# Rotary query halves swapped by transfers within SBUF, queries made three heads ahead

## The chip, the cores and the metric

The kernel runs on one core of a Trainium2 chip. The core has five engines that this text names: TensorE (PE, matrix products; its weight loads are listed apart as PEld), VectorE (DVE), ScalarE (ACT), GpSimd (POOL), and SyncE (SP), which in this kernel issues every transfer (DMA). Each engine works through its own queue in order; an instruction that waits holds up everything queued behind it on the same engine. Memory on the chip is SBUF (128 partitions) and PSUM, where PE leaves its sums.

The metric is the time of one execution in microseconds (us), median of several runs.

## The reference, cut to what matters

The reference is a two-block transformer with 4 sequences of 512 tokens and 1024 features: a first attention without weights, a mixture of low-rank experts, a second attention with low-rank queries and keys, and a second feed-forward. The change touches only the queries of the second attention, which has 32 heads:

```python
q = _rmsnorm(x @ wq_a.T, q_a_ln_w) @ wq_b.T
q = q.reshape(B, S, H, QHD)                       # 32 heads, 64 + 64 wide
q_nope, q_pe = (q[..., :NOPE], q[..., NOPE:])
q_pe = _apply_rope(_deinterleave(q_pe), cos, sin)  # x*cos + rotate_half(x)*sin
q_full = jnp.concatenate([q_nope, q_pe], axis=-1)
scores = jnp.einsum('bqhd,bkhd->bhqk', q_full, k_full) * softmax_scale
attn = jax.nn.softmax(where(causal, scores), axis=-1)
```

`rotate_half` takes 64 features to (minus the upper 32, the lower 32). For each of 32 heads and 4 sequences, a 64 x 512 block of the query is multiplied by a table of cosines, its two halves of 32 are exchanged and multiplied by a table of signed sines, and the two products are added.

## The kernel before

The kernel has four stages: the first attention, the first feed-forward, the heads of the second attention, and the second feed-forward (with the last output projection). The heads stage is a loop over 128 units `u`: 4 groups of 8 heads, 4 sequences per group, 8 heads each. A query lies transposed, 128 features on the partitions and 512 tokens along the free axis: features 0 to 63 are the part without rotation, 64 to 95 (`lo_`) and 96 to 127 (`hi_`) the two rotary halves, both together `mid`.

One query goes through these steps:

- `query(u)`: six matrix products of 512 columns (lines 150 to 152) leave it in the PSUM tile `psq`, of which there is one buffer. Every product of this kernel is made in three passes, from operands that are split into a high part and a low part.
- `rotate_query(u)`: ACT copies it to the SBUF tile `qf` (line 728, two buffers). DVE makes `t2` (the profile calls it `t`) from the PSUM tile with two multiplications of 32 partitions each, which read one half and write the other (lines 730 and 731). POOL multiplies `qf[mid]` by the cosines in place (line 732) and adds `t2` (line 733).
- `split_query(u)`: DVE casts columns 128 to 511 to the high part `qh` (line 740), POOL takes the low part `ql` by subtraction (line 741).
- `scores(u)`: four blocks of scores of 512, 384, 256 and 128 columns. The first product of each block reads `ql` (line 150), the last block reads `qf` (line 912). DVE adds the causal mask and takes the row minimum (line 918), ACT takes the exponential (line 921). The score tile `pss` has two buffers, so the third block waits until DVE is done with the first.
- `turn(u)` (line 942, copies at line 944) transposes the probabilities, `context(u)` (line 958, multiplication at 961) multiplies them by the keys' low-rank form for a pair of heads.
- `divisors(u)` sends the row sums through DRAM and back (`r_d`, `rb`, lines 887 and 891).

A "filler" is interleaved into the loop so that PE has work between the steps of a head: `project` (output projection of the previous sequence; operands added by DVE at line 984, cast by ACT at 992 and split by POOL into `cxl` at 993; sums added by DVE at 1035; its tiles `xs` loaded and stored by SP at lines 1020 and 1039) and `prepare_output` for the weights of a group.

The loop body of unit `u` has this order: two blocks of scores of `u`, a step of `context`, filler, `split_query(u + 1)`, two more blocks of scores, transposes of `u - 1`, filler, `query(u + 2)`, `rotate_query(u + 2)`, filler, transposes, and the loads: at the third head of a sequence `load_batch` fetches the next sequence's low-rank queries `q_d` (1 MB, line 699), keys `kT` (512 KB, line 701) and two smaller tensors. Queries 0 and 1 are made before the loop, at the end of the preceding projection stage; unit 0 makes query 2.

Inside this stage the order in each engine's queue isn't the written order: a planner simulates the program, keeps the data dependencies and lets an engine take the earliest written instruction that is ready by its own estimate of durations, transfers included. The order that results is then fixed; the engines wait by semaphores.

Of the kernel before, what the change touches and what calls it, by code (L numbers as in the profile page):

```python
# [17 lines left out]
P = 128  # L18
# [28 lines left out]
def block_kernel(ctx: ExitStack, tc: tile.TileContext, a: dict, out: bass.AP):  # L47
# [400 lines left out]
    wA = []  # L448

    def split_shared(pool, ch):  # L450
        r = rawA[:, ch * NA : (ch + 1) * NA]
        h, l = (pool.tile([P, NA], FR, name=f"wA{ch}{k}") for k in "hl")
        A.copy(h, r)
        G.tensor_tensor(l, r, f32(h), ALU.subtract)
        wA.append((h, l))
# [192 lines left out]
    ropeT = cc.tile([P, 2, S], F32, name="ropeT")  # L648
    nc.sync.dma_start(out=ropeT[NOPE:P], in_=a["ropeT"])
# [75 lines left out]
    def rotate_query(u):  # L725
        ps = queries[u]
        f = qp.tile([P, S], F32, name="qf")
        A.copy(f, ps)  # L728
        t2 = qp.tile([P, S], F32, name="t2", bufs=1)
        V.tensor_tensor(t2[lo_], ps[hi_], ropeT[hi_, 1, :], ALU.mult)  # L730
        V.tensor_tensor(t2[hi_], ps[lo_], ropeT[lo_, 1, :], ALU.mult)  # L731
        G.tensor_tensor(f[mid], f[mid], ropeT[mid, 0, :], ALU.mult)  # L732
        G.tensor_tensor(f[mid], f[mid], t2[mid], ALU.add)  # L733
        queries[u] = f

    def split_query(u):
        f = queries[u]
        h = qp.tile([P, S - P], FR, name="qh")
        l = qp.tile([P, S - P], FR, name="ql")
        V.tensor_copy(h, f[:, P:S])  # L740
        G.tensor_tensor(l, f[:, P:S], f32(h), ALU.subtract)  # L741
        queries[u] = f, h, l

    wqs, batches = {}, {}
    with tc.tile_pool(name="c1_w", bufs=1, side="right") as wap, \
# [73 lines left out]
        for s in range(NT + 1):  # L819
# [12 lines left out]
            if s in (NT - 2, NT - 1):  # L832
                query(s - NT + 2, pwp, "po")
                rotate_query(s - NT + 2)
# [10 lines left out]
    with ExitStack() as c2:  # L845
# [368 lines left out]
        for u in range(NU + 3):  # L1214
# [9 lines left out]
            if b == 0 and i == (HG // 2 if g else 0) and g < NG:  # L1224
                filler = prepare_output(g, wo_raw)
            sc = scores(u) if u < NU else iter(())
# [7 lines left out]
            if u + 1 < NU:  # L1234
                split_query(u + 1)

            if u == 0:
                query(2, psq, "psq")
            advance(sc)
# [10 lines left out]
            if 0 < u < NU - 2:  # L1250
                query(u + 2, psq, "psq")
            if u + 2 < NU:
                rotate_query(u + 2)
# [418 lines left out]
def _laid_out(i):  # L1672
# [8 lines left out]

    signed_T = np.concatenate([sin[:, :half], -sin[:, half:]], axis=1)
# [25 lines left out]
        "ropeT": np.stack([cos.T, signed_T.T], axis=1),  # L1708
# [21 lines left out]
```

## Time and profile before

| what | value |
|---|---|
| median of 3 runs | 1747.93 us (1747.41 to 1749.18) |
| span of the profiled execution, first to last instruction | 1746.3 us |
| heads stage in it (first rotated query's copy to the last unit's scores) | 414 to 1480 us |
| PE, DVE, ACT, POOL busy over the span | 98%, 75%, 52%, 53% |
| ACT copy of a query (line 728) | 587 ns, 126 of 128 from `psq` |
| DVE multiplications of the halves (730, 731) | 696 and 691 ns, 128 each |
| POOL cosine multiplication, addition, low part (732, 733, 741) | 1285, 1284 and 1013 ns, 128 each |

The profile is one execution of its own. Its page gives the span; its time from outside is the span and what lies around it, and isn't listed apart. The median of the three timed runs is 1.6 us above this span. Engines' busy times are sums of instructions; PE's instructions are pipelined and overlap, so a PE that is listed as busy can still lose time between two products. Waits are listed by the engine that stood still and the instruction that released it; "issue" means that nothing visible held it.

### The profile page before, as it was taken

What the parts mean: (1) busy time and instruction counts of PE and PEld (TensorE: products, weight loads), DVE (VectorE), ACT (ScalarE), POOL (GpSimd) and SP (SyncE); (2) the same over time, 40 slices, a digit from 0 to 9 for tenths busy, and PEclk for the clock granted to TensorE, in tenths of its full rate; (3) what the DMA queues carried; (4) which work ended last, traced back from release to release, by engine and by line L of the source; (5) the groups of instructions that cost most, each with busy time, mean ns of one, the idle gap of its engine ahead of it and who ended that gap; (6) DMA issues with size and microseconds to landing.
All of it is one profiled execution on the core that took longest, in us unless ns stands there. A gap on an engine that the chain in (4) does not pass through costs nothing.

```text
span 1746.3 us, 31628 instructions
## 1 busy us (share of the span) xinstructions
PE 1707.5 (98%) x10536; PEld 1429.7 (82%) x10536; DVE 1302.4 (75%) x3494; ACT 905.0 (52%) x2316; POOL 921.9 (53%) x926
## 2 busy tenths in 40 slices
PE   7999999999999999999999999999999999999999
PEld 6899999998677777767777767777767777789998
DVE  7977885676777777787777687777778776687675
ACT  7422331366765555575555575555476555453332
POOL 0553541203665665566566556566556655675454
PEclk9999999999999999999999999999999999999999
DMA  4313543245334234353333353342454333853431
GB/s 194 135 42 115 185 159 114 89 138 169 106 99 140 81 118 140 113 172 117 110 112 119 110 193 95 106 139 94 131 169 151 102 110 109 309 201 123 137 105 74
DMA packets 131939, 228.16 MB, mean 131 GB/s; under 512 B 22272, under 2 KB 58752, under 8 KB 128448
## 3 DMA queue, kind: packets, MB, share of 16 engines
q1 hardware_dynamic: 131776, 226.13, 39.2%
q8 instruction: 84, 1.38, 0.3%
q14 instruction: 79, 0.65, 0.1%
HBM read 156.60 MB, written 71.83 MB: 131 GB/s over the span
## 4 chain that ended last, share of the span: by engine, by line
PE 88%; DVE 5%; POOL 4%; ACT 2%; issue 1%; DMA 0%; POOLq 0%; ACTq 0%; DVEq 0%
PE psv L958 8%; PE pst L942 7%; PE po L150 4%; PE po L152 4%; PE po L151 4%; PE pss L150 4%; PE pss L151 3%; PE pss L152 3%; PE pob L150 3%; PE poa L150 3%; PE psq L150 3%; PE psq L152 3%; PE psq L151 3%; PE acc L150 3%; PE acc L152 3%; PE acc L151 3%
## 5 line engine op out<-in xcount | busy, mean ns | idle before, releaser
L921 ACT ACTIVATE p<-p,mn 128x512 f32<-128x512 f32 (+3 forms) x512 | 284.9, 559 | 211.4 <-DVE mn L918 210.8
L732 POOL TENSOR_TENSOR qf<-qf,ropeT 64x512 f32<-64x512 f32 x128 | 164.4, 1285 | 259.1 <-ACT qf L728 249.3
L918 DVE CUSTOM_DVE_ANT_0 p<-pss,causal 128x512 f32<-128x512 f32 (+3 forms) x512 | 232.7, 485 | 19.8 <-PE pss L152 15.8
L942 PE MATMUL pst<-ident,p 128*128 128x128 f32 x1280 | 185.9, 273 | 1.8 <-ACT pT L944 1.7
L733 POOL TENSOR_TENSOR qf<-qf,t 64x512 f32<-64x512 f32 x128 | 164.3, 1284 | 32.0 <-DVE t L731 23.8
L942 PEld LDWEIGHTS pst<-ident,p 128*128 128x128 f32 x1280 | 153.0, 141 | 29.6 <-ACT pT L944 4.8
L944 ACT COPY pT<-pst 128x512 f32<-128x512 f32 x256 | 142.1, 579 | 31.4 <-PE pst L942 29.5
L741 POOL TENSOR_TENSOR ql<-qf,qh 128x384 fp32r<-128x384 f32 x128 | 129.6, 1013 | 53.0 <-DVE qh L740 53.0
L150 PE MATMUL pss<-kT,ql 128*128 128x512 f32 (+2 forms) x384 | 143.6, 374 | 4.4 <-POOL ql L741 4.2
L993 POOL TENSOR_TENSOR cxl<-s,cxh 128x256 fp32r<-128x256 f32 x128 | 98.1, 773 | 85.2 <-ACT cxh L992 53.9
L150 PE MATMUL po<-w_h,hTl 128*128 128x384 f32 (+1 forms) x384 | 133.1, 347 | 0.7 <-DVE x L433 0.6
L151 PE MATMUL pss<-kT,qh 128*128 128x512 f32 (+2 forms) x384 | 130.4, 340 | 0.0
L152 PE MATMUL po<-w_h,hTh 128*128 128x384 f32 (+1 forms) x384 | 130.1, 339 | 0.0
L152 PE MATMUL pss<-kT,qh 128*128 128x512 f32 (+2 forms) x384 | 129.9, 338 | 0.0
L151 PE MATMUL po<-w_l,hTh 128*128 128x384 f32 (+1 forms) x384 | 129.7, 338 | 0.0
L944 DVE COPY pT<-pst 128x256 f32<-128x256 f32 x128 | 54.1, 423 | 97.8 <-PE pst L942 97.2
L728 ACT COPY qf<-psq 128x512 f32<-128x512 f32 x126 | 73.9, 587 | 69.7 <-PE psq L152 68.0
L730 DVE TENSOR_TENSOR t<-psq,ropeT 32x512 f32<-32x512 f32 x126 | 87.7, 696 | 24.5 <-ACT qf L728 20.2
L921 ACT ACTIVATION_READ_ACCUMULATOR p<-p,mn 128x1 f32 x512 | 97.2, 190 | 0.0
L150 PEld LDWEIGHTS pss<-kT,ql 128*128 128x128 f32 x384 | 72.1, 188 | 29.1 <-POOL ql L741 9.2
L731 DVE TENSOR_TENSOR t<-psq,ropeT 32x512 f32<-32x512 f32 x126 | 87.1, 691 | 1.7
L1035 DVE TENSOR_TENSOR xs<-xs,pob 128x512 f32<-128x512 f32 x105 | 71.1, 677 | 19.0 <-PE pob L152 18.8
(567 smaller groups left out, 4975.0 us busy)
## 6 DMA issues: line engine op xcount, KB each, us to landing
xs<-x_d SPq DMA_DIRECT2D x128, 256.0 KB
x_d<-xs SPq DMA_DIRECT2D x128, 256.0 KB
slotC<-in_woT_dram SPq DMA_DIRECT2D x32, 512.0 KB
rb<-r_d SPq DMA_DIRECT2D x128, 128.0 KB
w_t<-raw SPq DMA_DIRECT2D x32, 288.0 KB
x<-in_x_dram SPq DMA_DIRECT2D x16, 512.0 KB
x_d<-x SPq DMA_DIRECT2D x32, 256.0 KB
slotA<-q_d SPq DMA_DIRECT2D x8, 1024.0 KB
```

The source lines that it names most:

```text
L150: T.matmul(ps, lhsT=al, rhs=bh, start=start, stop=False, **kw)
L151: T.matmul(ps, lhsT=ah, rhs=bl, start=False, stop=False, **kw)
L152: T.matmul(ps, lhsT=ah, rhs=bh, start=False, stop=stop, **kw)
L732: G.tensor_tensor(f[mid], f[mid], ropeT[mid, 0, :], ALU.mult)
L733: G.tensor_tensor(f[mid], f[mid], t2[mid], ALU.add)
L741: G.tensor_tensor(l, f[:, P:S], f32(h), ALU.subtract)
L918: turn_of[0] = V.tensor_tensor_reduce(out=to, in0=ps[:, 0:n], in1=causal[:, S - n : S], scale=1.0, scalar=-NEG, op0=ALU.add, op1=ALU.min, ...
L921: A.activation(to, to, AF.Exp, bias=mn[:, i : i + 1], scale=-1.0, accum_out=rs[:, i : i + 1])
L942: T.transpose(ps[:, w : w + P], p[:, OF[i] + j * P : OF[i] + (j + 1) * P], ident)
L944: copy(pT[:, AT[js[0]] : AT[js[0]] + w], ps[:, 0:w])
L958: T.matmul(ps[n * KVR : (n + 1) * KVR, S - w : S], lhsT=k[:, j, :], rhs=pTs[u + n][:, AT[j] : AT[j] + w], start=(j == 0), stop=(j == TPB - 1))
L993: G.tensor_tensor(l, src, f32(h), ALU.subtract)
```

## The change

- `ropeT` is now laid out over 128 partitions: the signed sines on partitions 0 to 63, the cosines on 64 to 127 (256 KB as before).
- `rotate_query` exchanges the halves by two transfers from `qf` to partitions 0 to 63 of `t2`, 32 partitions of 2 KB each (64 KB per transfer), issued on SP. One DVE multiplication then reads `t2[0:64]` and the sines, both in SBUF, and writes `t2[64:128]`. POOL's cosine product goes to a tile of its own, and POOL adds the two products into `qf`. The PSUM tile is read by ACT alone.
- `qf` has three buffers. The loop makes and rotates `query(u + 3)` in unit `u` (unit 0 makes queries 2 and 3), and `split_query(u + 1)` stands ahead of the scores of `u`.
- The POOL tile shares its place with the weight tile `wA0` of the projection stage, whose two halves become one tile.

```diff
     def split_shared(pool, ch):
         r = rawA[:, ch * NA : (ch + 1) * NA]
-        h, l = (pool.tile([P, NA], FR, name=f"wA{ch}{k}") for k in "hl")
+        both = pool.tile([P, 2, NA], FR, name=f"wA{ch}")
+        h, l = both[:, 0], both[:, 1]
...
-    ropeT = cc.tile([P, 2, S], F32, name="ropeT")
-    nc.sync.dma_start(out=ropeT[NOPE:P], in_=a["ropeT"])
+    ropeT = cc.tile([P, S], F32, name="ropeT")
+    nc.sync.dma_start(out=ropeT, in_=a["ropeT"])
...
-    def rotate_query(u):
+    def rotate_query(u, pool=None):
         ps = queries[u]
-        f = qp.tile([P, S], F32, name="qf")
+        f = qp.tile([P, S], F32, name="qf", bufs=3)
         A.copy(f, ps)
         t2 = qp.tile([P, S], F32, name="t2", bufs=1)
-        V.tensor_tensor(t2[lo_], ps[hi_], ropeT[hi_, 1, :], ALU.mult)
-        V.tensor_tensor(t2[hi_], ps[lo_], ropeT[lo_, 1, :], ALU.mult)
-        G.tensor_tensor(f[mid], f[mid], ropeT[mid, 0, :], ALU.mult)
-        G.tensor_tensor(f[mid], f[mid], t2[mid], ALU.add)
+        nc.sync.dma_start(out=t2[0:32], in_=f[hi_])
+        nc.sync.dma_start(out=t2[32:NOPE], in_=f[lo_])
+        V.tensor_tensor(t2[mid], t2[0:NOPE], ropeT[0:NOPE], ALU.mult)
+        tc_ = (pool or firstp).tile([P, S], F32, name="wA0", bufs=1)
+        G.tensor_tensor(tc_[mid], f[mid], ropeT[mid], ALU.mult)
+        G.tensor_tensor(f[mid], tc_[mid], t2[mid], ALU.add)
         queries[u] = f
...
                 query(s - NT + 2, pwp, "po")
-                rotate_query(s - NT + 2)
+                rotate_query(s - NT + 2, wk)
...
+            if u + 1 < NU:
+                split_query(u + 1)
             sc = scores(u) if u < NU else iter(())
...
             advance(filler, per[0])
-            if u + 1 < NU:
-                split_query(u + 1)
 
             if u == 0:
                 query(2, psq, "psq")
+                rotate_query(2)
...
-            if 0 < u < NU - 2:
-                query(u + 2, psq, "psq")
-            if u + 2 < NU:
-                rotate_query(u + 2)
+            if u + 3 < NU:
+                query(u + 3, psq, "psq")
+                rotate_query(u + 3)
...
-        "ropeT": np.stack([cos.T, signed_T.T], axis=1),
+        "ropeT": np.concatenate([signed.T, cos.T]),
```

## The prediction

> **What bounds the kernel now.** I read the page's first and fourth parts, then the heads stage alone: busy time by stretch, the waits of PE and of its weight loads, the instructions on the query's tiles, and SP's waits.
>
> ```profile
> span 1746.3 us, 31628 instructions
> PE 1707.5 (98%) x10536; PEld 1429.7 (82%) x10536; DVE 1302.4 (75%) x3494; ACT 905.0 (52%) x2316; POOL 921.9 (53%) x926
> PE 88%; DVE 5%; POOL 4%; ACT 2%; issue 1%; DMA 0%; POOLq 0%; ACTq 0%; DVEq 0%
> ```
>
> PE is busy nearly all the time, and 88% of the chain that ended last runs on it. The second answer is a table by stretch (stretch, length, then busy time and instruction count of PE, PEld, DVE, ACT, POOL):
>
> ```profile
> 465.00:700.00 235.00, 232.78 (x1307) 178.07 (x1306) 175.40 (x474) 136.05 (x377) 143.92 (x140) 1.00 0.36 116
> 940.00:1200.00 260.00, 258.84 (x1432) 197.00 (x1431) 193.89 (x513) 152.39 (x416) 158.54 (x155) 1.00 0.38 122
> ```
>
> In the heads stage PE is idle 2.2 us in 235 and 1.2 us in 260. So nothing that DVE, POOL or ACT saves is time in itself; only what makes PE wait counts. The weight-load and matmul waits of the stage (414 to 1480 us; total, times, longest):
>
> ```profile
> PEld pss L150 <- POOL ql L741: 9.2, 23, 1.5
> PEld pst L942 <- ACT pT L944: 4.4, 6, 0.8
> PEld pob L150 <- POOL cxl L993: 3.8, 12, 0.7
> PE pss L150 <- POOL ql L741: 4.2, 8, 1.2
> PE pst L942 <- ACT pT L944: 1.7, 4, 0.4
> PE pob L150 <- POOL cxl L993: 0.9, 3, 0.3
> ```
>
> The largest wait with a named cause is the first: a head's scores stand still for `ql`, the low part of their query. The timeline shows why: POOL makes `ql` at 914.19 to 915.20 us, and the scores that read it start at 915.25. The query's chain ends just in time.
>
> **The change, part by part.** The sum is made against the profiled span, 1746.3 us; the median of the runs is 1.6 us above it, and I add that at the end.
>
> *A query made three heads ahead.* 118 query copies lie between 465 and 1466 us: 1001/118 = 8.5 us per head. The rotation moves a head forward and the split to the start of the preceding head. Every instruction of the rotation moves with it: the ACT copy, the transfers, the DVE multiplication, both POOL operations; six products on PE are made earlier, not more often. `ql` then has about 8.5 us to spare less what the new chain takes longer (below). The waits for `ql`: 9.2 us of weight loads, in the same places as the 4.2 us of matmuls, so between 4.2 and 13.4; I take 9.2, because a held weight load delays the product by itself. From 465 us on 6.1 us of it lie (19 times), before that 3.1 us (4 times). Gain: 6.1 in the steady part. What is late next there is `cxl` (3.8 + 0.9 us listed, and 1.9 on the other output bank), which this part doesn't help.
>
> *The start.* Queries 0 and 1 gain no lead: their rotation is still the last thing before their scores. Of the 3.1 us before 465, I let 1.5 go (heads 2 to 5, which do gain) and charge heads 0 and 1 for the longer chain.
>
> *The transfers.* SP issues 2 more transfers per query, 256 in all; transfer issues here take 0.33 us (`x_d` stores) to 0.54 us (`rb`), so 0.66 to 1.08 us per query and 84 to 138 us of SP's time. SP waits far longer than that:
>
> ```profile
> SPq L887 <- DVE rt L883: 171.6, 56, 10.3
> SPq L1039 <- DVE mn L918: 142.9, 29, 11.6
> SPq L699 <- PE psv L958: 104.5, 14, 9.6
> SPq L1020 <- DMA x_d<-xs: 61.9, 60, 3.4
> ```
>
> (465 to 1466 us.) Behind the new issues stand loads and stores of `xs`, the `r_d`/`rb` round trip and the batch loads. They come up to 1.1 us later. `rb` of one pair is issued at 908.69 and multiplied in by DVE at 919.10, the `xs` loads stand still for earlier stores anyway. I take 0, with 0 to +3 us as its ends: were that cover gone, 1.1 us on each of some three dozen `xs` loads would show through 0.1 us at a time.
>
> No row shows how long a transfer inside SBUF takes. The nearest is `r_d`: its fourth issue ends at 924.27 and the `rb` issue, which waits for it, starts at 925.23, so at most 0.96 us to land 1 KB. For 128 KB I add 0.4 us at the fastest slice of the page (309 GB/s) to 1.0 us at its mean (131 GB/s). Issue and landing together: 2.0 to 3.0 us behind the copy, if nothing larger is in front; a 1 MB `q_d` load in front adds up to 1024 KB/309 GB/s = 3.4 us, a 512 KB load 1.7 us. A landing at once would be the other end; 2.3 us is what I take, nearest to the `r_d` row.
>
> *One multiplication instead of two.* The rows (min/median/max ns):
>
> ```profile
> L730 DVE TENSOR_TENSOR t<-psq,ropeT x126: 695/696/697, 426.1 to 1468.6; 32x512 f32<-32x512 f32 x126
> L731 DVE TENSOR_TENSOR t<-psq,ropeT x126: 690/691/692, 426.8 to 1469.3; 32x512 f32<-32x512 f32 x126
> L984 DVE TENSOR_TENSOR s<-a,a x16: 679/811/1328, 1506.8 to 1718.0; 128x512 f32<-128x512 f32 x16
> ```
>
> Two times 0.69 = 1.39 us go, each with one operand in PSUM and a flat duration. The new one has both operands in SBUF; the nearest row for that form and length is the third, 0.68 to 1.33 us, median 0.81. Saved per head: 0.06 to 0.71 us, I take 0.55; over 128 heads 70 us of DVE's time, 8 to 91 as ends. It is hidden, since DVE isn't the bound. What it moves: now the mask of the first score block stands behind both multiplications (908.61 + 0.69, then the mask at 909.33, although its scores were done near 908.1), and the third block's products wait for that mask. Waits of weight loads on DVE in the whole stage are small (mask 2.6 and 2.4 us, `cx` 2.4, `rt` 2.4), together 9.8 us. I take a gain of 2, between 0 and 9.8.
>
> The SBUF page of the Trainium skill ("SBUF — State Buffer", section "Who interferes with whom") speaks against this edit: a Vector instruction with two SBUF inputs contends with a GpSimd instruction that reads SBUF, one with at most one such input doesn't. The spread of the third row beside the flat first two agrees. By its exclusive lock the new multiplication could stand behind a whole POOL operation and take 1.28 us more, which would make the pair's replacement dearer than the pair by about 0.6 us per head. The rows' bound above doesn't need it.
>
> *POOL* has the same three instructions per head, 1285 + 1284 + 1013 ns; the added tile changes no size. `t2` is ready 2.3 + 0.8 = 3.1 us after the copy instead of 1.6 us (copy ends 907.87, second multiplication 909.30), so the addition starts some 1.5 us later. In the steady part that is paid from the 8.5 us. For heads 0 and 1 it is paid in full: 2 x 1.5 = 3, less what PE can fill in with query 2 or 3; the second also has a 1 MB and a 512 KB load in front of it (issued at 416.80 and 418.32, its copy near 420). I take +2, ends 0 and 5.
>
> *What queues behind the new wait.* On DVE the multiplication waits for the landing, and masks, casts, sums and copies stand behind it; on POOL the addition waits for DVE, with `cxl` and `ql` behind. The planner puts both where its own estimate lands the transfer, so only a later landing costs, and a mask has the 1.39 us of the removed multiplications to give. I take +2 for landings behind big loads; ends 0 and +23, the latter worked out as the first rival.
>
> Sum: -6.1 - 1.5 + 2 - 2 + 0 + 2 = -5.6, so a span of 1740.7 and a median of about 1742.5 us. The ends that lower it: 13.4 instead of 7.6 for `ql`, 9.8 instead of 2 for DVE.
>
> **The rivals.** First, slower: *DVE stands on the swap.* Large loads in the stage: 16 of 1 MB, 16 of 512 KB keys, 32 of 512 KB `slotC`. If a swap meets one, it lands 3.4 or 1.7 us late. Less 1.4 us of slack that is 2.0 and 0.3 us at DVE's queue: 16 x 2.0 + 48 x 0.3 = 46 us if all meet, 23 us if half do, and PE, which has no reserve, shows it. 1742.5 - 2 + 23 = 1763.5. For it: PE's few waits mean that every new one counts, and SP stands still two thirds of the time (its eleven largest waits sum to 667 of 1001 us), so a swap could also queue behind a store that isn't ready (up to 11.6 us). Against it: DVE is idle a quarter of the stage, its own waits there (94 us on transposes) cost PE almost nothing. It decides once DVE's lateness costs PE more than the 7.6 us gained: 0.06 us per head.
>
> Second, no difference: *the wait is replaced.* `ql` is no longer late, but `cxl` is, since POOL's addition now lies about where `cxl` is split (the split at 911.97 would fall into an addition from about 911.0 to 912.3). 0.3 us more on a third of the 128 units, less those with spare operands: +5, so 1747.5. For it: 6.6 us of such waits are there already. Against it: the filler makes its operands two steps ahead.
>
> Third, a larger gain: *all named waits shrink.* `ql` 13.4, DVE 9.8 by half, `cxl` by half: 13.4 + 4.9 + 6.6/2 - 2 (the charge at the start) = 19.6 at most, 14 more than the forecast's 5.6; half way there is 1742.5 - 7 = 1735.5. For it: DVE loses 70 us of work, and the query's PSUM tile is free after the copy, so the planner can fill PE's gaps with a query. Against it: PE's idle time in the steady stretches is barely 6 us in 1001.
>
> **How the numbers follow.** 0.2%, 3.5 us, is about what a measurement of this kernel can tell from no change: below 1744.4 is faster, above 1751.4 slower. Chances: forecast 0.42, DVE stands on the swap 0.34, wait replaced 0.14, larger gain 0.10. The forecast's own range is 1737 to 1746.5; a fifth of it (0.08) lies within 3.5 us of before, and of the slow rival 0.02 does. Faster 0.34 + 0.10 = 0.44; same 0.14 + 0.08 + 0.02 = 0.24; slower 0.32. The range of 8 in 10 leaves out the lower half of the larger gain (0.05) and the slow rival beyond its worked price (0.13): 1734 to 1764.
>
> **What would show it.** Right: the wait of the scores on `ql` gone but for the first two heads; DVE busy down by about 70 us in the heads stage and its multiplication near 0.8 us; the mask of the first block no longer behind a multiplication; PE's busy time unchanged, the stage shorter by 4 to 8 us. Wrong: DVE idle in front of the new multiplication, released by the transfer, for more than 1 us in many heads; masks late behind it and weight loads of the third score block waiting on them; or `cxl` waits above 10 us. The prediction fails most easily by the landing time of the swap, which no row shows.

## The result and the profile after

The changed kernel takes 1773.66 us (median of 4 runs, 1773.17 to 1775.28) beside 1748.33 us for the kernel before on the same chip: 1.0145 times as long, 95% interval 1.0133 to 1.0158. The forecast was 1742.5 us in a range of 1734 to 1764; it was wrong in sign, and the time lies 9.7 us above the range.

The page's first part and the chain, after:

```profile
span 1771.4 us, 32282 instructions
...
PE 1703.4 (96%) x10536; PEld 1431.8 (81%) x10536; DVE 1246.9 (70%) x3366; ACT 907.9 (51%) x2316; POOL 939.5 (53%) x926
...
PE 59%; POOL 5%; DVE 4%; issue 2%; DMA 1%; ACT 1%; SPq 0%; POOLq 0%; ACTq 0%; DVEq 0%
```

DVE lost 55.5 us of work, as the edit promised. PE is no busier, yet the span is 25.1 us longer: PE stood still. The shares of the chain that are listed sum to 72%, so I read from it only that PE's listed share fell from 88 to 59%.

Two tables by stretch show where (stretch, length, busy time and instruction count of PE, PEld, DVE, ACT, POOL, then the granted clock, the DMA share and GB/s). Before, for the start of the heads stage, which the prediction didn't show:

```profile
414.00:465.00 51.00, 48.09 (x264) 34.36 (x263) 37.55 (x117) 37.14 (x101) 31.44 (x28) 1.00 0.45 140
```

After:

```profile
421.00:465.00 44.00, 34.36 (x160) 23.96 (x161) 21.50 (x71) 24.31 (x65) 19.82 (x17) 0.92 0.36 105
465.00:700.00 235.00, 230.21 (x1315) 176.82 (x1315) 163.04 (x455) 141.79 (x389) 153.21 (x143) 1.00 0.42 133
784.30:799.60 15.30, 12.18 (x58) 9.02 (x58) 10.38 (x23) 8.77 (x21) 10.80 (x11) 0.89 0.31 97
800.00:1030.00 230.00, 228.50 (x1285) 178.85 (x1285) 158.02 (x425) 126.65 (x352) 144.07 (x140) 1.00 0.43 134
```

PE idles 9.6 us in the first 44, 3.1 us in 15 around 790, and 1.5 us in the 230 us after that. The loss is in a few places. To see them all, I take for each head the time of its last score product (line 915 after, 912 before) and subtract the same of the kernel before. The lag is 5.2 us at head 0, 16.0 at head 9, then falls to 13.0 at head 43, is 19.0 at head 47, 23.2 at head 79, 28.1 at head 111, and 24.6 at the last. So there is a start that costs 16 us, three jumps between heads 43 and 47, 75 and 79, 107 and 111, each at the same head of a group, and between them a slow gain. At the start and at the jumps the filler is `prepare_output`: the output weights of a group are made from loads into `slotC`, on PE, ACT, DVE and POOL.

What PE and its weight loads waited for from 421 to 1480 us (total, times, longest):

```profile
PE pss L150 <- POOL ql L744: 21.9, 12, 3.4
PE pss L150 <- DVE mn L921: 9.9, 10, 2.7
PE pob L150 <- POOL cxl L996: 1.6, 3, 0.6
PEld pss L150 <- POOL ql L744: 26.7, 18, 3.7
PEld pss L150 <- DVE mn L921: 15.1, 19, 3.1
```

The scores wait for `ql` in fewer places than before (18 weight loads instead of 23), but for three times as long in all, and for a mask that is late, which they hardly did before:

```profile
PEld pss L150 <- DVE mn L918: 2.6, 7, 0.8
```

`cxl` is not late.

What DVE, POOL and SP waited for in the same time:

```profile
DVE qh L743 <- POOL qf L736: 114.8, 119, 2.0
DVE t L733 <- DMA t<-qf: 13.7, 19, 1.7
POOL qf L736 <- DVE t L733: 54.9, 51, 3.8
SPq L731 <- ACT qf L729: 115.9, 55, 4.7
SPq L731 <- POOL qf L736: 70.2, 30, 6.6
SPq L1049 <- PE pst L945: 10.3, 4, 3.3
```

The second line is the wait that the first rival was built on. It is small: DVE met an unfinished transfer 19 times, 1.7 us at most. The swap is late further up, on SP: 30 times it waits for POOL's addition (line 736), since `t2` has one buffer and the addition is its last reader. The sixth line is a load into `slotC` that waits for its room, and the jump at head 44 shows what that does. SP's queue there (start, duration, issue):

```profile
772.65 0.97 SPq L890 DMA_DIRECT2D r_d<-rt  x3
776.66 0.83 SPq L1049 DMA_DIRECT2D slotC<-in_woT_dram  x2
...
778.45 0.51 SPq L731 DMA_DIRECT2D t<-qf  x1
...
788.64 0.54 SPq L731 DMA_DIRECT2D t<-qf  x1
```

ACT's copy of query 44 ended at 772.50. SP stood 3 us on the `slotC` load, issued it, and reached the swap at 778.45, 5.95 us behind the copy. What followed on DVE, POOL and PE:

```profile
786.42 0.69 DVE L733 TENSOR_TENSOR t<-t,ropeT 64x512 f32<-64x512 f32 x1
...
787.32 1.29 POOL L736 TENSOR_TENSOR qf<-wA,t 64x512 f32<-64x512 f32 x1 [3.00 <-PE pst L945]
788.65 0.36 DVE L743 CAST qh<-qf 128x384 fp32r<-128x384 f32 x1 [0.82 <-POOL qf L736]
...
788.70 1.45 POOL L735 TENSOR_TENSOR wA<-qf,ropeT 64x512 f32<-64x512 f32 x1
790.22 1.26 POOL L1091 TENSOR_TENSOR b221l<-raw,b221h 128x512 fp32r<-128x512 f32 x1
791.45 0.99 POOL L744 TENSOR_TENSOR ql<-qf,qh 128x384 fp32r<-128x384 f32 x1
...
792.49 0.50 PE L150 MATMUL pss<-kT,ql 128*128 128x512 f32 x1 [3.12 <-POOL ql L744]
```

The multiplication stands in DVE's queue behind a head's masks and divisors and runs 7.4 us after the start of the swap's second issue; the addition frees `t2` at 788.61 and the next swap is issued 0.03 us later; `ql` stands on POOL behind the next query's cosine product and a weight's low part; PE stands 3.12 us. From copy to the end of `ql` this took 19.9 us, where the kernel before took 5.4. Every step is an engine that works its queue in order, and every wait is handed on.

### The profile page after: what moved, and what is told of

Read it like the earlier page. It is cut to its first block, busy times and chain, and to the rows that moved or that the text cites. A ratio compares the mean times of both kernels' runs of the same rounds, so it can differ in the third digit from the quotient of the medians.

```text
span 1771.4 us, 32282 instructions
## 1 busy us (share of the span) xinstructions
PE 1703.4 (96%) x10536; PEld 1431.8 (81%) x10536; DVE 1246.9 (70%) x3366; ACT 907.9 (51%) x2316; POOL 939.5 (53%) x926
## 4 chain that ended last, share of the span: by engine, by line
PE 59%; POOL 5%; DVE 4%; issue 2%; DMA 1%; ACT 1%; SPq 0%; POOLq 0%; ACTq 0%; DVEq 0%
PE psv L961 8%; PE pst L945 6%; PE pss L150 4%; PE pss L151 3%; PE pss L152 3%; PE pob L150 3%; PE poa L150 3%; PE psq L152 3%; PE psq L150 3%; PE psq L151 3%; PE acc L150 3%; PE acc L152 2%; PE acc L151 2%; PE poa L152 2%; PE poa L151 2%; PE pob L152 2%
## 5 line engine op out<-in xcount | busy, mean ns | idle before, releaser
L736 POOL TENSOR_TENSOR qf<-wA,t 64x512 f32<-64x512 f32 x128 | 165.0, 1289 | 115.5 <-DVE t L733 54.9
L735 POOL TENSOR_TENSOR wA<-qf,ropeT 64x512 f32<-64x512 f32 x128 | 169.4, 1323 | 58.4 <-ACT qf L729 50.2
L151 PE MATMUL pss<-kT,qh 128*128 128x512 f32 (+2 forms) x384 | 133.0, 346 | 0.0
L152 PE MATMUL pss<-kT,qh 128*128 128x512 f32 (+2 forms) x384 | 131.2, 342 | 0.0
L743 DVE CAST qh<-qf 128x384 fp32r<-128x384 f32 x128 | 46.1, 360 | 116.9 <-POOL qf L736 116.9
L733 DVE TENSOR_TENSOR t<-t,ropeT 64x512 f32<-64x512 f32 x128 | 109.0, 852 | 19.0 <-DMA t<-qf 15.2
L996 POOL TENSOR_TENSOR cxl<-cx,cxh 128x256 fp32r<-128x256 f32 x96 | 76.8, 803 | 84.9 <-ACT cxh L995 78.8
```

The costliest lines, as they stand in the source:

```text
L151: T.matmul(ps, lhsT=ah, rhs=bl, start=False, stop=False, **kw)
L152: T.matmul(ps, lhsT=ah, rhs=bh, start=False, stop=stop, **kw)
L735: G.tensor_tensor(tc_[mid], f[mid], ropeT[mid], ALU.mult)
L736: G.tensor_tensor(f[mid], tc_[mid], t2[mid], ALU.add)
L996: G.tensor_tensor(l, src, f32(h), ALU.subtract)
```

## The experiments

All times are medians; "before" is 1747.7 to 1748.8 us in all groups. The reference in the tables is the second kernel of the first group, 1742.86 us: three heads ahead, rotation as before. Lags are differences of the last score product of a head between two profiled executions.

### Which part costs

Three parts can be taken one by one: the rotation (new: transfers and one multiplication; old: two multiplications out of PSUM), the heads of lead, and the place of the split. With the old rotation and a third `qf`, the sines were put on partitions 0 to 63 to make room.

The split put back:

```diff
-            if u + 1 < NU:
-                split_query(u + 1)
             sc = scores(u) if u < NU else iter(())
...
             advance(filler, per[0])
+            if u + 1 < NU:
+                split_query(u + 1)
```

> The changed kernel with the split of the next query put back behind the second score block, where it was before; transfers, one multiplication and three heads ahead stay. Theory S (the cast, queued ahead of the masks, makes VectorE stand on GpSimd's addition: 116.9 us of such waits against 15.1 before): the stand falls to under 40 us, the start's loss of 16 us and most of the three jumps of 6.6 us go, the small steady gain stays: 1735 to 1750. Theory R (the rotation by transfers is what comes late: the swap waits for the one buffer t2, and the addition stands in GpSimd's queue): 1765 to 1780, as the changed kernel (1773.7). Theory L (three heads ahead by itself upsets the order): the same 1765 to 1780.

The lead taken back to two heads, besides:

```diff
             if u == 0:
                 query(2, psq, "psq")
-                rotate_query(2)
...
-            if u + 3 < NU:
-                query(u + 3, psq, "psq")
-                rotate_query(u + 3)
+            if 0 < u < NU - 2:
+                query(u + 2, psq, "psq")
+            if u + 2 < NU:
+                rotate_query(u + 2)
```

> Transfers and the one multiplication alone: queries two heads ahead and the split at its old place. S: no early cast, so no loss but also little lead for ql; 1742 to 1752. R: the longer rotation has now one head less of lead, so its lateness shows in full: 1775 to 1800, TensorE waiting on ql for over 60 us. L: 1742 to 1752.

The old rotation with the new lead and split, and with the old split:

```diff
-        f = qp.tile([P, S], F32, name="qf")
+        f = qp.tile([P, S], F32, name="qf", bufs=3)
...
-        V.tensor_tensor(t2[lo_], ps[hi_], ropeT[hi_, 1, :], ALU.mult)
-        V.tensor_tensor(t2[hi_], ps[lo_], ropeT[lo_, 1, :], ALU.mult)
-        G.tensor_tensor(f[mid], f[mid], ropeT[mid, 0, :], ALU.mult)
+        V.tensor_tensor(t2[lo_], ps[hi_], ropeT[0:32], ALU.mult)
+        V.tensor_tensor(t2[hi_], ps[lo_], ropeT[32:NOPE], ALU.mult)
+        G.tensor_tensor(f[mid], f[mid], ropeT[mid], ALU.mult)
```

> The two multiplications out of PSUM of the kernel before, with no transfers, but queries three heads ahead and the split ahead of the scores (the sine rows stand in partitions 0 to 63 to make room for the third query). S: VectorE stands on the addition as in the changed kernel and the time is 1762 to 1780. R: with no transfers the addition is not late: 1740 to 1750. L: 1762 to 1780.

> The rotation of the kernel before, split at its old place, only the queries made three heads ahead. S and R: 1742 to 1750, within 0.4% of before. L: 1762 to 1780.

| rotation | lead | split | time, us | ratio to before, 95% |
|---|---|---|---|---|
| old | 3 | early | 1742.86 | 0.9962 (0.9949 to 0.9975) |
| old | 3 | late | 1742.25 | 0.9961 (0.9947 to 0.9975) |
| new | 3 | early (the change) | 1773.66 | 1.0145 (1.0133 to 1.0158) |
| new | 3 | late | 1776.73 | 1.0158 (1.0143 to 1.0173) |
| new | 2 | late | 1943.55 | 1.1102 (1.1072 to 1.1132) |

Theories S and L fall: the early split costs nothing, and three heads of lead alone gain 6 us. The new rotation costs 31 us with three heads of lead and 195 us with two. Theory R, which is left, expected 1775 to 1800 us for two heads and missed that by 144 us: the scores' first products wait 135.9 us for `ql` there (89 times, 5.6 us at most, 421 to 1660 us), and the kernel falls behind in the steady stretches too (13 us from head 20 to head 40). The kernel with the old rotation and the lead beats both kernels of this study; its scores no longer wait for `ql` (0.4 us of weight loads in all; before, 9.2). Its page:

```profile
span 1740.0 us, 31730 instructions
...
PE 1700.4 (98%) x10536; PEld 1429.2 (82%) x10536; DVE 1304.6 (75%) x3494; ACT 903.3 (52%) x2316; POOL 925.4 (53%) x926
```

### What of the rotation costs

Four runs take the rotation apart: a second buffer for `t2`, a control for the room that it needs, no transfers (the halves are then not exchanged), and transfers that nobody waits for.

```diff
-        t2 = qp.tile([P, S], F32, name="t2", bufs=1)
+        t2 = qp.tile([P, S], F32, name="t2", bufs=2)
...
-            junk = wk.tile([P, QR], F32, name="junk")
+            junk = wk.tile([P, QR], F32, name="junk", bufs=1)
...
-        xsp = c2.enter_context(tc.tile_pool(name="c2_x", bufs=5, side="right"))
+        xsp = c2.enter_context(tc.tile_pool(name="c2_x", bufs=4, side="right"))
```

> The changed kernel with two buffers for t2, so that the swap of a query need not wait for GpSimd's addition of the query before; room for it from four instead of five xs tiles and one instead of two junk tiles. Theory B (the one buffer closes a loop: swap, landing, multiplication, addition, next swap; in the changed kernel 58 of 127 swaps start 0.03 us behind the preceding addition, mostly in the start and at the three jumps): 1740 to 1755, swaps starting at the preceding addition under 15 times. Theory Q (the multiplication's place in VectorE's queue, up to 7 us behind the landing, is what is late, whatever the buffer): 1764 to 1776. Theory C (the transfers and SyncE's issues by themselves cost): 1764 to 1776.

The control has the last two edits and one `t2`.

> Control: the changed kernel with one t2, and the four xs tiles and one junk tile of the run with two t2. All theories: 1770 to 1780, as the changed kernel; what it differs by is the price of the room.

```diff
-        nc.sync.dma_start(out=t2[0:32], in_=f[hi_])
-        nc.sync.dma_start(out=t2[32:NOPE], in_=f[lo_])
-        V.tensor_tensor(t2[mid], t2[0:NOPE], ropeT[0:NOPE], ALU.mult)
+        V.tensor_tensor(t2[mid], f[0:NOPE], ropeT[0:NOPE], ALU.mult)
```

> The changed kernel without the two transfers: the multiplication reads the query's first 64 partitions instead of the swapped halves, so the rotation's sine part is left wrong. One multiplication, three heads ahead and the early split stay. B: the loop shrinks to multiplication and addition, 1738 to 1746. Q: with no landing to plan for, the multiplication stands where the two stood before, 1738 to 1746. C: 1738 to 1746. If it stays above 1760, the transfers are not the cause at all, but the one multiplication out of SBUF or the product's own tile.

To the reference kernel:

```diff
         t2 = qp.tile([P, S], F32, name="t2", bufs=1)
+        if u >= 2:
+            d = firstp.tile([P, S], F32, name="wA0", bufs=1)
+            nc.sync.dma_start(out=d[0:32], in_=ropeT[hi_])
+            nc.sync.dma_start(out=d[32:NOPE], in_=ropeT[lo_])
```

> The rotation of the kernel before (two multiplications out of PSUM), three heads ahead, split early, and beside it two transfers per query of the same size within SBUF, from the rotary table into a tile that nobody reads: traffic and SyncE's issues without the dependence. B and Q: 1741 to 1747. C: 1760 to 1775.

| kernel | time, us | ratio, 95% |
|---|---|---|
| two `t2` | 1772.04 | 1.0141 (1.0126 to 1.0156) |
| control, one `t2`, same room | 1788.82 | 1.0236 (1.0221 to 1.0251) |
| no transfers | 1750.71 | 1.0016 (1.0006 to 1.0025) |
| dead transfers, old rotation | 1743.53 | 0.9974 (0.9965 to 0.9983) |

Theory C falls: 252 transfers of the same size, issued by SP and written at the same place in the loop, cost 0.7 us when nobody waits for them. (As they wait for no copy, they run ahead of their heads: the last is issued at 1145 us, some 310 us before the last query's copy ends, so there are none at the third jump; at the first two there are.) The loss comes from waiting for the swap: without the transfers 23 us are gone. Every theory expected more of that, 1738 to 1746. Theory B expected 1740 to 1755 for two `t2` and missed (theory Q's 1764 to 1776 fits); the control was expected at 1770 to 1780 and took 1788.82. The second buffer does gain 16.8 us on its control, but the room for it costs 15 us, mostly in heads 1 to 9, so it is worth something only there. (Of the 58 swaps that the expectation names, 31 start within 0.06 us of the preceding addition, the rest within 0.6 us. With two buffers there are none.) At the jumps nothing improves: the swap of heads 43 to 46 is issued 1.5 us behind the copy on the mean instead of 5.5, yet `ql` ends 17.3 us behind it instead of 17.9. What is gained on SP is lost on DVE and POOL.

The run without transfers also held a surprise: with one multiplication it takes 8 us more than the reference does with two. The rows of POOL's cosine product in it, and in a later run whose multiplication reads PSUM:

```profile
L733 POOL TENSOR_TENSOR wA<-qf,ropeT x128: 1268/1730/1794, 415.5 to 1463.9; 64x512 f32<-64x512 f32 x128
```

```profile
L733 POOL TENSOR_TENSOR wA<-qf,ropeT x128: 1267/1284/1303, 413.6 to 1452.3; 64x512 f32<-64x512 f32 x128
```

The edit of that later run, and what it was expected to do:

```diff
-        V.tensor_tensor(t2[mid], f[0:NOPE], ropeT[0:NOPE], ALU.mult)
+        V.tensor_tensor(t2[mid], ps[0:NOPE], ropeT[0:NOPE], ALU.mult)
```

> The changed kernel without transfers, its one multiplication reading the unswapped halves straight out of PSUM (the sine part is left wrong): what one multiplication in place of two is worth at best. Theory K (the multiplication out of SBUF beside GpSimd made the run without transfers 8 us slower than two multiplications, GpSimd's cosine product taking 1668 ns on the mean instead of 1284): 1736 to 1743. If the 8 us have another source (the product's own tile, the order): 1748 to 1752.

It took 1740.41 us (0.9956, 0.9941 to 0.9972): theory K holds. Beside a DVE instruction with two SBUF inputs, POOL's product takes 1730 ns at the median instead of 1284. The two runs differ in that operand alone, their multiplications start alike (0.2 and 0.1 us behind ACT's copy, means of 126 heads), and the times lie 10 us apart. One multiplication in place of two is worth 2.4 us at best, in the form that reads PSUM, within what these intervals can tell apart from nothing.

### Does another queue or another place help

```diff
-        nc.sync.dma_start(out=t2[0:32], in_=f[hi_])
-        nc.sync.dma_start(out=t2[32:NOPE], in_=f[lo_])
+        nc.scalar.dma_start(out=t2[0:32], in_=f[hi_])
+        nc.scalar.dma_start(out=t2[32:NOPE], in_=f[lo_])
```

> The changed kernel with the two transfers issued by ScalarE, which makes the copy that they read, instead of SyncE. Theory S (SyncE's queue: with two t2 the swap of head 44 still started 6.0 us behind its copy, because SyncE stood 3 us on the load of the next output weights, which waits for its room, and on the divisors' store; this explains the three jumps and part of the start): the jumps of 6.6 us go and the time falls to 1745 to 1760; the single t2 can make ScalarE stand, and 256 issues of 0.55 us load it with some 140 us more, so not all of the 31 us need come back. Theory Q (the multiplication's place in VectorE's queue): nothing changes, 1768 to 1785. Theory B alone (one buffer): ScalarE now stands in SyncE's stead, with masks' exponentials behind it, 1775 to 1800.

> As the run with ScalarE's transfers, and two buffers for t2 (four xs tiles, one junk tile). S and B together: nothing is left that holds a swap back, 1742 to 1752. S alone: as with one t2, 1745 to 1760. Q: 1765 to 1785.

> The changed kernel with the two transfers issued by GpSimd, which makes the addition that frees t2, so that no swap waits for another engine's queue except for the copy. S: jumps gone, 1748 to 1765, GpSimd paying for the issues. Q: 1768 to 1785.

The third has `nc.gpsimd` in place of `nc.scalar`. Then the second half of the rotation was written a head later:

```diff
+    def turn_query(u, pool=None):
+        f, t2 = queries[u]
+        V.tensor_tensor(t2[mid], t2[0:NOPE], ropeT[0:NOPE], ALU.mult)
+        tc_ = (pool or firstp).tile([P, S], F32, name="wA0", bufs=1)
+        G.tensor_tensor(tc_[mid], f[mid], ropeT[mid], ALU.mult)
+        G.tensor_tensor(f[mid], tc_[mid], t2[mid], ALU.add)
+        queries[u] = f
...
             advance(filler, per[0])
+            if 0 < u < NU - 2:
+                turn_query(u + 2)
```

> The changed kernel with the rotation cut in two: copy and transfers stay where they are, the multiplication, the cosine product and the addition of that query are written in the next head, behind its second score block. Theory L (what costs is the transfer's latency inside one chain of in-order queues: copy, issue, landing, multiplication, addition, cast; the head of lead is spent behind the chain instead of inside it): the transfer now has half a head, no engine meets it, and the three jumps and the start come back: 1736 to 1746, VectorE standing before the multiplication under 5 us. Theory K (the one multiplication itself, which reads two operands from SBUF beside GpSimd; without transfers the time was still 1750.7): 1747 to 1756. Theory X (anything else of the transfers): 1765 to 1780.

> As before, but the second half of the rotation is written at the beginning of the next head, ahead of its scores. L: nearly as good, 1736 to 1750; where the transfer lands behind large loads some stall may remain. K: 1747 to 1756. X: 1765 to 1780.

> As the one with the second half at the beginning of the next head, with the transfers issued by ScalarE. L: 1736 to 1750, within 4 us of the same with SyncE. K: 1747 to 1756. X: 1762 to 1780.

Means over heads 43 to 46 (the first jump), from the end of ACT's copy to the start of the first swap issue, to the multiplication (the reference's second), and to the end of `ql`, and the lag behind the reference at heads 9, 40, 47 and 127, all us:

| kernel | time | swap | mult. | `ql` end | lag 9 | 40 | 47 | 127 |
|---|---|---|---|---|---|---|---|---|
| reference | 1742.86 | - | 1.4 | 7.1 | 0 | 0 | 0 | 0 |
| the change | 1773.66 | 5.5 | 12.4 | 17.9 | 17.1 | 14.2 | 20.6 | 31.0 |
| two `t2` | 1772.04 | 1.5 | 10.7 | 17.3 | 11.4 | 9.0 | 16.2 | 26.2 |
| ACT issues | 1770.14 | 0.9 | 6.6 | 10.6 | 10.6 | 8.6 | 15.5 | 27.1 |
| ACT issues, two `t2` | 1769.85 | 0.6 | 6.2 | 10.2 | 10.4 | 8.9 | 15.0 | 24.8 |
| POOL issues | 1789.69 | 1.3 | 5.6 | 11.7 | 12.4 | 16.7 | 23.7 | 47.8 |
| second half a head later | 1773.38 | 5.5 | 12.6 | 18.0 | 15.2 | 12.3 | 19.1 | 30.2 |
| the same, ahead of the scores | 1774.25 | 5.5 | 12.6 | 18.0 | 16.0 | 13.2 | 20.1 | 30.5 |
| that with ACT's issues | 1768.78 | 0.7 | 6.1 | 10.0 | 10.8 | 8.8 | 14.8 | 26.5 |

Theory S fell too: it expected 1745 to 1760 for ACT's issues, 1742 to 1760 for them with two `t2`, and 1748 to 1765 for POOL's, which took 1789.69, above every theory's range. By the times theory Q fits ACT's runs (1768 to 1785, 1765 to 1785), but it says that the multiplication stands far behind the landing, and with ACT's issues DVE reaches it before the landing at 49 heads, at the first head of each jump by 3 us. With ACT's issues the swap is hardly late, the chain at the jumps is 7 us shorter, and the scores' weight loads wait 0.9 us in all for `ql`. The start gets better, but the jumps stay as large: 6.9 us from head 40 to 47 with ACT's issues, 6.4 in the changed kernel. They have another cause now, the one that the first rival named. At the first jump, SP and ACT's first issue, then DVE, and then PE:

```profile
763.87 0.33 SPq L700 DMA_DIRECT2D slotA<-q_d  x1
764.15 0.51 ACTq L731 DMA_DIRECT2D t<-qf  x1
...
770.07 0.69 DVE L733 TENSOR_TENSOR t<-t,ropeT 64x512 f32<-64x512 f32 x1 [3.24 <-DMA t<-qf]
770.79 0.69 DVE L1094 TENSOR_TENSOR b111l<-poa,b111h 128x512 fp32r<-128x512 f32 x1
...
771.53 1.83 PE L1071 MATMUL poa<-slotC 128*64 128x512 f32 x4 [2.24 <-DVE b111l L1094]
```

ACT issued this swap at 764.15 and 764.70, and it landed some 4.8 us behind the second issue's end, where 1.5 us is the least. SP had issued the 1 MB load of `q_d` 0.28 us ahead of it, and that load was moved first: none of the swap's packets were moved before 768.0 us, while 1.01 MB of SP's were from 764.0 on. That is 3.3 us later than the least, and the rival's price for such a load was 3.4 us. DVE stood 3.24 us on it, with the low part of an output weight behind it, and PE needed that weight's PSUM tile. `DVE t <- DMA` grew from 13.7 us to 58 us in all (49 times, 3.5 us at most).

The three kernels with the second half a head later took the times of theory X, but they say nothing on theory L: with SP's issues the multiplication still starts 12.6 us behind the copy (12.4 in the change), with ACT's 6.1 (6.6). The planner orders by when operands are ready by its own estimate, so the written place moves little. That may also be why the split's place made little difference. An order that forces the multiplication behind other work on DVE wasn't tried.

### Are the large loads the cause

Of the four loads of output weights per group of heads, this edit leaves only the first pair's; the 1 MB loads of `q_d` and the keys stay.

```diff
-                if half and n + 1 < len(prs):
+                if False:
                     fetched = fetch_output(g, prs[n + 1])
```

> The changed kernel with the output weights of only the first pair of heads of each group loaded (the other three pairs reuse them, so the output is left wrong): 12 of the 16 loads of 1.15 MB into slotC are gone, and with them SyncE's wait for the room and the transfers that the swap can land behind. Theory D (those loads, ahead of the swap on SyncE's queue and on the transfer engines, are what holds the rotation back where the output weights are prepared): the three jumps of 6.6 us and some of the start go, 1746 to 1757. Theory E (in these stretches every engine's queue is a dense chain, and the four or five steps that the rotation has more, engine to engine, hold it up whatever is loaded): 1766 to 1775.

> Control: the two multiplications out of PSUM, three heads ahead, with the same loads left out. Both theories: 1738 to 1744, as with all loads (1742.9).

> The changed kernel with both suspected holds taken away at once: the transfers issued by ScalarE, and only the first of four output-weight loads per group (output left wrong, as in the run with SyncE's transfers). If the start's heads 1 to 9 (12 us) are lost on SyncE's queue and t2, and the jumps (20 us) to the loads, the two add up: no jump over 2 us, heads 1 to 9 within 4 us of the kernel with two multiplications, and only the 5 to 8 us of head 0 stay: 1746 to 1756. If the two are one and the same cost that only changes its place, 1757 to 1766.

| kernel | time, us | ratio, 95% | lag 9 | 40 | 47 | 79 | 127 |
|---|---|---|---|---|---|---|---|
| the change, a quarter of the loads | 1759.07 | 1.0064 (1.0046 to 1.0082) | 17.3 | 15.0 | 16.0 | 15.4 | 18.4 |
| reference, a quarter of the loads | 1749.73 | 1.0009 (0.9999 to 1.0018) | -0.2 | 0.6 | 1.1 | 2.3 | 4.1 |
| ACT issues, a quarter of the loads | 1770.88 | 1.0138 (1.0121 to 1.0155) | 10.6 | 12.5 | 18.9 | 24.7 | 28.1 |

For the changed kernel theory D holds at the jumps: the first two are gone (15.0, 16.0, 15.4) and the third is 4 us instead of 7; the start stays, and the time lies 2 us above theory D's range. Less its control, its loss is 9 us by the medians (14 by the profiles) instead of 31. The control itself was expected at 1738 to 1744, and its 7 us more than the reference with all loads I can't explain.

With ACT's issues the same loads left out bring nothing. The time lies above both ranges that the expectation gave, the jumps are back, and PE waits for DVE again (421 to 1480 us):

```profile
PE poa L150 <- DVE t41l L1094: 10.7, 3, 4.0
PE pss L150 <- DVE mn L921: 8.0, 4, 6.4
```

In it DVE stands 3.2 us on the transfer at head 44 and 3.3 us at head 76, which land 5.2 and 5.3 us behind their second issue's end. What lies in front of them is one of the loads that are left, the first pair's for the next group, which SP issues as soon as its room is free. At head 44, SP, ACT, DVE and PE:

```profile
776.65 0.36 SPq L1049 DMA_DIRECT2D slotC<-in_woT_dram  x1
776.77 0.52 ACTq L731 DMA_DIRECT2D t<-qf  x1
783.08 0.68 DVE L733 TENSOR_TENSOR t<-t,ropeT 64x512 f32<-64x512 f32 x1 [3.20 <-DMA t<-qf]
784.54 0.79 PE L150 MATMUL poa<-b110h,cxl 128*128 128x512 f32 x1 [3.93 <-DVE t41l L1094]
```

The 512 KB load is issued 0.12 us ahead of the swap (0.15 us at head 76), and none of the swap's packets were moved before 779.2 us. So in this run the load is not gone from in front of the swap that matters. It doesn't tell whether the two holds add up or are one cost that changes its place: the expectation's question stays open, and a kernel with ACT's issues and nothing in front of the swap wasn't tried.

### What is settled

Shown: the lead gains 6 us; the transfers cost next to nothing as traffic or as issues; the query's dependence on them costs 23 us against the same written order without them, 33 against the best form of one multiplication (the planner's order changes with each edit, so these are differences of whole kernels); most of it falls where the output weights are prepared; with SP's issues the loads of these weights make the first two jumps and part of the third. Read from the traces, not tested by a run: on SP it is the queue ahead of the swap, on ACT it is DVE's stand on a swap that lands behind a large load. Open: which order of the queues would keep it off PE, and whether anything is left of the jumps when no load precedes the swap.

About 5 of the start's 17 us have nothing to do with the transfers. The kernels without transfers have them too, 6.7 and 5.6 us at head 0. In the first of these the trace says why:

```profile
430.10 0.69 DVE L919 CUSTOM_DVE_ANT_0 p<-pss,causal 128x512 f32<-128x512 f32 x1 [2.59 <-DMA kT_d<-kT]
```

Head 0's first mask waits for a store of the stage before. The tile of POOL's product adds 2 KB per partition to that stage's pool, and I take it that the place of `p` then overlaps a tile that is still being stored. With one junk tile less (two `t2`, its control, ACT with two `t2`) head 0 is at -1.3, 1.0 and -1.8 us. That is argued from the addresses' order, not shown. Nor would mending it alone gain these 5 us by this record: in the same three kernels head 2 is 5.0 to 5.5 us late all the same.

## Why the prediction was wrong

*Three heads ahead* (-6.1 - 1.5, of which +2 back at the start). Right, mechanism and size: -5.9 and -6.5 us measured, the waits on `ql` gone.

*One multiplication instead of two* (-2, DVE -70 us). Wrong for the form that the change has: without transfers, the multiplication out of SBUF takes 7.9 us more than the two do; only the form that reads PSUM gives the -2, with -2.4 us. DVE's busy time fell by 55.5 us in the change, within the ends given. The duration, 0.81 us forecast, was 852 ns on the mean:

```profile
L733 DVE TENSOR_TENSOR t<-t,ropeT x128: 684/686/1622, 417.4 to 1490.1; 64x512 f32<-64x512 f32 x128
```

What the forecast left out is the other side of the contention: it priced a longer DVE instruction, and no longer POOL instruction; the run without transfers shows POOL's product 446 ns longer at the median. The exclusive lock of the Trainium skill's "SBUF — State Buffer" ("Who interferes with whom") agrees, and the prediction had cited it and then set it aside ("The rows' bound above doesn't need it").

*The landing* (2.3 us behind the copy, "the prediction fails most easily" by it). Right where nothing is in front: the multiplication of head 41 starts 2.8 us behind the copy, 2.2 us behind the second issue's start. This was not what failed in the changed kernel.

*The issues on SP* (0, 0 to +3). This step failed. It counted what stands behind the new issues and found it covered, which the dead transfers confirm. It didn't count what stands ahead of them; the first rival names it in half a sentence and without a price. The lines were there: SP's waits in the prediction's fourth fence, up to 11.6 us, were read as room, and a queue that waits two thirds of its time is the opposite of room for a transfer that another engine needs. The Trainium skill states the rule ("DMA: Bandwidth & Descriptors", "Anatomy of one DMA — SWDGE (gpsimd) path"): a transfer's semaphore waits happen on the sequencer that issues it, before it is sent (it stands there beside the path that GpSimd issues). Here SP stood 3 us on a `slotC` load with the swap behind it.

*`t2`'s one buffer* isn't in the prediction at all. Before, `t2` was written from 0.2 us behind the copy and freed 3.0 us later (means of 126 heads). With a transfer in it, the time from the first swap issue to the end of the addition is 6.6 to 11.4 us for heads 2 to 6 and 44 and 45, as long as a head, and 30 swaps wait 70 us for it.

*"The planner puts both where its own estimate lands the transfer, so only a later landing costs"* (+2, 0 to +23). This step failed with the one above, and it is the term that was mis-sized: 31 us less the 5 of head 0 (and with the start's part, which the prediction charged apart) instead of 2. The estimate fixes an order, and an order that counts on the landing makes every engine behind it late by what SP, DVE or POOL is late. Eight and a half us "to spare" were real in the steady stretches (there `ql` ends 9.0 us after the copy, the heads come as fast as in the reference), and not where the chain took 18.

*The start* (+2, 0 to +5). Wrong: 16 us, of which 5 lie at head 0 and the rest in heads 1 to 9. There the loop through `t2` and SP takes 6.5 to 11.4 us, where heads followed each other in about 7 us before. It is not the whole: with two `t2` and ACT's issues the lag at head 9 is still 10.4 us instead of 17.1, and what makes that isn't shown.

*The rivals.* "DVE stands on the swap" had the sign, the place (where large loads are) and nearly the size: 23 us against 31. In the changed kernel the stand is on SP and POOL, DVE's is 13.7 us; moved to ACT's queue, it becomes DVE's as described (58.2 us). That the rival's size comes near in the changed kernel is therefore partly luck: it was worked out for a stand of DVE behind loads on the transfer engines, and the change lost on the issuing queue. Its chance of 0.34 was too small: "against it" I set that DVE idles a quarter of the stage and that its waits cost PE almost nothing, and an average over the stage says nothing on the stretches where DVE frees PSUM tiles that PE needs next. "The wait is replaced by `cxl`" didn't come (1.6 us), and neither did the larger gain; PE's 6 us of idle time spoke rightly against that.

## What to carry to other kernels

A transfer put into a chain of engines that are all near their limit is priced by what stands ahead of it on the queue that issues it, by what is being moved when it is sent, by how long its target buffer is now held, and by what stands behind each engine that waits, not by its bytes or its issue. Look for the stretches in which those queues are dense, not for the mean. A longer lead is worth having for itself, but it doesn't pay for a longer chain if one single-buffered tile or one in-order queue ties consecutive rounds together: take the lead alone.

## What the hardware showed that I hadn't expected

A stand of PE costs more than its length. After the 3.12 us at the jump the granted clock fell to half:

```profile
786.00:792.40 6.40, 3.37 (x21) 2.32 (x17) 4.82 (x10) 3.98 (x8) 4.92 (x5) 1.00 0.13 28
792.40:796.00 3.60, 3.51 (x10) 2.98 (x11) 2.09 (x3) 1.82 (x4) 2.81 (x4) 0.56 0.38 137
796.00:799.60 3.60, 3.60 (x22) 3.10 (x21) 2.76 (x7) 1.89 (x5) 3.05 (x4) 0.96 0.42 130
```

(The granted clock is the third figure from the end: 1.00, 0.56, 0.96.) In these 3.6 us PE made 10 products; those of 512 columns took 0.63 us and followed each other at 0.42 us, instead of 0.40 and 0.23. So by my estimate (half the clock for some 3.4 us) the stand of 3.1 us cost about 1.7 us more, which a sum of waits doesn't contain. The page "TensorE: Matmul & The Clock Gate" of the Trainium skill ("What's actually happening") gives the same pattern: half the clock after an idle window of about 3.4 us, and as long again until it is full. Here shorter stands were enough: 3.12 us, and in the run with ACT's issues 2.24 us, after which the granted clock was 0.50 from 771.8 to 775.1 us.

A DVE instruction with two SBUF inputs and a POOL instruction hold each other up, and the one that started first keeps its own duration. In the run without transfers DVE's multiplication started 0.05 to 0.12 us ahead of POOL's product at 98 of 128 heads: it took 684 to 686 ns, the product 1712 to 1794. At 16 heads the product had started first, by 0.3 to 0.9 us: it took 1268 to 1300 ns, the multiplication 922 to 1512. With one input in PSUM the same DVE instruction stayed within 683 to 687 ns, the product within 1267 to 1303.
